# A two-layer graph network on one core: edge weights of the second layer by halves of the partitions, and one-hot products for more blocks of edges

## The chip, the core and the metric

The kernel runs on one NeuronCore of a Trainium2 chip. The core has five engines, each with its own instruction queue, which meet only through semaphores: TensorE (PE in the profile; its weight loads are listed apart as PEld), VectorE (DVE), ScalarE (ACT), GpSimd (POOL) and SyncE (SP), which here only issues transfers. TensorE writes to PSUM, which has eight banks of 2 KB per partition. The metric is the device time of the whole program in microseconds; the time before is the median of three runs.

## The reference

There are 6,250 nodes with 128 features and 200,000 directed edges, sorted by their receiving node. Each layer is added to its input.

```python
h = maximum(layernorm(x), 0)
# layer one: attention over the incoming edges, 8 heads of 16
z = (h @ W).reshape(N, 8, 16); el = einsum(z, attn_l); er = einsum(z, attn_r)
e = leaky_relu(el[src] + er[dst]);  a = exp(e - segment_max(e, dst)[dst])
x = x + segment_sum(z[src] * a, dst) / segment_sum(a, dst) + bias

h = maximum(layernorm(x), 0)
# layer two: s are the first 32 features, v the other 96 as 32 x 3
s, v = s @ W_up_s / sqrt(32), einsum(v, W_up_v) / sqrt(32)
t = silu(silu(edge_attr_8 @ A1 + b1) @ A2 + b2) @ A3        # 128 weights per edge
w0, w1, w2, w3 = split(t, 4)
m = concat(s[src] * y_s * w0, (v[src] . y_v) / sqrt(3) * w3,
           s[src] * y_v * w1, v[src] * y_s * w2)             # 256 per edge
x = x + (segment_sum(m, dst) / 10) @ W_out
```

Everything is float32.

## The kernel before

**Tiles and blocks.** 128 edges are a tile, one edge per partition; 16 tiles (KB) are a block. There are 1,563 tiles in 98 blocks (NB), the last of 11 tiles. Block b writes to a window of 128 nodes, of which the first 64 are complete when it ends; the other half is carried to the next block (`carry`). Two blocks complete one tile of 128 nodes, of which there are 50 (NX).

**Rows of the source nodes.** Each tile needs, for each of its 128 edges, the row of its source node: 136 numbers from table t0 in layer one, 128 from t1 in layer two. There are three ways to get them.

- A *gather*: one indirect DMA per tile, issued by GpSimd (`gather`, line 839).
- *By row*: for the last tile of every third block, SP issues 128 small DMAs with addresses from registers (`rows_by_row`, line 1154). ScalarE copies the result to its place (`filled`).
- *Products*: for the tile before the last (KD) of the blocks in `dense` (layer one, line 1200) or `dense1` (layer two, line 1201), TensorE multiplies one-hot matrices by a copy of the whole table that lies in SBUF as three bfloat16 parts (`t0s`, `t1s`). That takes 51 matmuls (`rows_of`, line 1313; `dense_rows`, line 1917), two wide comparisons on VectorE and three operations that pick the right range.

In layer one the copy of the table is read back in 17 chunks of three node tiles: `asked(k)` issues the DMA on SP, and `split(k)` makes the three parts on VectorE. Both have two buffers.

**The prologue.** Node tiles are loaded in ten groups, normalised, transposed and multiplied by W to give t0. Most of the normalising subtraction is on VectorE; in the groups before the last two, some tiles are given to GpSimd (line 960). The first KX = KB + 9 = 25 tiles of edges are gathered from x itself, before t0 is there (line 905), and go through the same arithmetic again, tile by tile (`rows_of` of the prologue with `raw`).

**Layer one** runs a loop over groups g (a group is a block; the last block is two). Step g works on the logits of block g, on the weights and sums of block g - 1 (`sums`, line 1427), and on the rows of blocks g + 1 and g + 2. At the end of each odd block a node tile is finished, and its rows are written to t1 (line 1495) and, all but the last three node tiles, to a second table t1z.

**Between the layers.** The first NE = 24 tiles of layer two are gathered from t1z, which lacks the last three node tiles, so they need not wait for them. `late_ends` and `late_rows` add what is missing by one-hot matmuls, four tiles at a time. All later gathers need t1 complete.

**Layer two** runs a loop over steps of four tiles (`us`), four per block. In step i of block b the order is:

1. at a block's start: gathers of block b + 2, rows of `filled`, features and attributes of block b + 2 (`edge_rows`: ft and yb), node rows;
2. `network(b + 1, ...)`: one of four parts of the two-layer network of the next block, through bank p_h (lines 1770 and 1774, Silu on ScalarE);
3. `tensor_weights` of step i + 1: two tiles of edges share the 128 partitions of h2, 64 each, so that one matmul per pair with a block-shaped a3p of 256 columns gives the weights p_w of both (line 1787); ScalarE scales two quarters of them (line 1791);
4. `messages` of step i on VectorE, lines 1807 to 1816;
5. products for this or the next block (`dense_step`), late rows, the one-hot matrix `s` of step i + 1;
6. if the step before ended a block: `finish` (VectorE adds the carry, ScalarE copies the next one), and one step later `node1`;
7. `sums1` of step i (line 1824), into bank p_u.

The order on PE, VectorE, ScalarE and SP is as written, by hand (`manual_schedule`). GpSimd issues nothing but gathers, into a ring of five buffers of a block each (`buffers`), plus z_first. In layer two p_h, p_w and p_u have two banks each, p_x and p_i one.

Of the kernel before, what the change touches and what calls it, by code (L numbers as in the profile page):

```python
# [9 lines left out]
F32 = mybir.dt.float32  # L10
# [3 lines left out]
OP = mybir.AluOpType  # L14
# [4 lines left out]
P = 128  # L19
# [5 lines left out]
MU = 32  # L25
# [716 lines left out]
def tile_even_edges(  # L742
# [62 lines left out]
    ok_i = keep.tile([1, 1], I32, name="fok")  # L805
    KX = KB + 9
    z_second = keep.tile([P, KB, ZW], F32, name="fz_second")
# [48 lines left out]
    with tc.manual_schedule(engines={mybir.EngineType.PE, mybir.EngineType.DVE,  # L856
# [81 lines left out]
        def rows_of(gx, xs, fp, fp_ps, raw=None):  # L938
# [5 lines left out]
            for k in range(NC + 3):  # L944
# [3 lines left out]
                if 0 <= c < NC:  # L948
                    i, n = gx[c]
                    rs, mr = rss[c], mrs[c] = normal(fp, mvs[c], rss[c], n, f"x{mark}{i}")  # L950
                    h = hs[c] = fp.tile([P, 6, P], F32, name="fh")
                    for j in range(n):
                        by = (i + j) % 7
                        if by in ((2, 6) if c < NC - 2 else (2,)):
                            nc.scalar.activation(h[:, j, :], xs[c][:, j, :], AF.Identity,
                                                 bias=mr[:, j, :], scale=rs[:, j, :])
                        else:
                            late = by in (0, 3, 5) and NC - 4 <= c < NC - 2 and not raw
                            eng = nc.gpsimd if late else nc.vector
                            eng.tensor_scalar(h[:, j, :], xs[c][:, j, :], mvs[c][:, j, 0:1],  # L960
                                              rs[:, j, :], op0=OP.subtract, op1=OP.mult)
                if k == NC + 1 and not raw:
# [48 lines left out]
def even_edges(tc, v):  # L1011
# [8 lines left out]
    with ExitStack() as ctx:  # L1020
# [27 lines left out]

        NL, NE = 3, 24
        LATE = NX - NL  # L1050
# [81 lines left out]
        a1p = const.tile([P, KB // 2, P], F32, name="fa1p")  # L1132
        nc.sync.dma_start(a1p, v["a1p"])
        a2p = const.tile([P, P], F32, name="fa2p")
# [43 lines left out]
        def finish(b, p_u, width, carry, agg, pool):  # L1178

            if b % 2 == 0:  # L1180
                agg = pool.tile([P, MW], F32, name="agg")
            o = agg[b % 2 * WB : b % 2 * WB + WB, :width]
            if carry is None:
                nc.vector.tensor_copy(o, p_u[:WB, :width])
            else:
                nc.vector.tensor_add(o, p_u[:WB, :width], carry[:, :width])
            carry = pool.tile([WB, MW], F32, name="carry")
            nc.scalar.copy(carry[:, :width], p_u[WB:, :width])
            return carry, agg

# [8 lines left out]
        TS = 3  # L1199
        dense = set(range(-(-NX // TS) + 4, NB - 4))  # L1200
        dense1 = set(range(10, NB - 4, 4))

# [35 lines left out]
        with tc.manual_schedule(engines=in_order), \  # L1238
# [338 lines left out]
            for g in range(NG - 3):  # L1577
# [5 lines left out]
                for n in split_:  # L1583
                    parts_out(n)
                asked(g - 2)
                if g % 2 == 0 and g // 2 + 2 < NX - 2:
# [68 lines left out]
                if to:  # L1655
                    rows_of(n2, 6, half - 6)
                split(g - 3)
                if g == 4:
# [76 lines left out]
        with tc.manual_schedule(engines=in_order), \  # L1735
# [11 lines left out]
            def edge_rows(b):  # L1747
                if b < NB:
                    c = blk[b]
                    c["ft"] = l1.tile([P, P], F32, name="ft", bufs=4)  # L1750
                    nc.sync.dma_start(c["ft"], f8[:, b, :])
                    c["yb"] = l1.tile([P, KB, 4], F32, name="yb", bufs=4)
                    nc.sync.dma_start(c["yb"], y4[:, b * KB : (b + 1) * KB, :])

            def network(b, step):

                c = blk[b]
                q0, second = step // 2 * 4, step % 2
                if 2 * q0 >= KT[b]:
                    return  # L1760
                if step == 0:
                    c["h2"] = []
                if step == 3 or 2 * q0 + 8 >= KT[b] and second:
                    c["yp"] = held[:, P + b % 2 * KB * 3 : P + (b % 2 + 1) * KB * 3].rearrange(
                        "p (t i) -> p t i", i=3)
                    nc.scalar.copy(c["yp"], c["yb"][:, :, 1:4])  # L1766
                p_h = l1_ps.tile([P, 4, P], F32, name="p_h")
                if not second:
                    for q in range(4):
                        nc.tensor.matmul(p_h[:, q, :], a1p[:, q0 + q, :], c["ft"], start=True, stop=True)  # L1770
                    c["h1"] = l1.tile([P, 4, P], F32, name="h1")
                    nc.scalar.activation(c["h1"], p_h, AF.Silu, bias=b1)  # L1772
                else:
                    nc.tensor.matmul(p_h.rearrange("p q e -> p (q e)"), a2p,  # L1774
                                     c["h1"].rearrange("p q e -> p (q e)"), start=True, stop=True)
                    h2 = l1.tile([P, 4, P], F32, name="h2", bufs=5)
                    nc.scalar.activation(h2, p_h, AF.Silu, bias=b2)  # L1777
                    c["h2"].append(h2)

            def tensor_weights(u):  # L1780

                b, k0, m = u["b"], u["k0"], u["m"]
                c = blk[b]
                w = u["w"] = l1_ps.tile([P, 4, 4, MU], F32, name="p_w")
                for k in range(0, m, 2):
                    q, n = (k0 + k) // 2, min(2, m - k)
                    nc.tensor.matmul(w[:, k : k + n].rearrange("p k a u -> p (k a u)"),  # L1787
                                     c["h2"][q // 4][:, q % 4, :],
                                     a3p[:, :n].rearrange("p k f -> p (k f)"), start=True, stop=True)
                for k in range(m):  # L1790
                    nc.scalar.activation(w[:, k, ::2, :], w[:, k, ::2, :], AF.Copy,  # L1791
                                         scale=c["yb"][:, k0 + k, 0:1])

            def messages(u):
                b, k0, m, w = u["b"], u["k0"], u["m"], u["w"]
# [67 lines left out]
            def late_ends(t):  # L1863

                if t < NE:
                    p_h = l1_ps.tile([P, 4, P], F32, name="p_h")
                    for k in range(4):
# [60 lines left out]
            def dense_step(b, q):  # L1928
# [6 lines left out]
                if b in dense1:  # L1935
# [17 lines left out]

            rows, rows_until.n, late, x_of = rows_by_row(1, t1, P), 0, [], {}
            for b in range(2):
                edge_rows(b)
                take_rows(b)
# [8 lines left out]
            carry = agg = None  # L1966
            ends = None
            for i, u in enumerate(us):
                b, k0, m = u["b"], u["k0"], u["m"]
                if k0 == 0:  # L1970
                    take_rows(b + 2)
                    filled(1, b, blk[b]["z"], P)
                    edge_rows(b + 2)
                    if b % 2 == 0:
                        node_rows1(b // 2, 1 if b < NB - 2 else 2)
                    table_tiles(b)
# [8 lines left out]
                late_ends(4 * (i + 2))  # L1985
                messages(u)
                if i == 26:
# [30 lines left out]
            nc.vector.tensor_copy(m_t[:, 2:], p_n[:, 2:])  # L2018
            p_o = l1_ps.tile([P, 4, P], F32, name="p_w")
            for j in range(2):  # L2020
                for q in range(2):
                    nc.tensor.matmul(p_o[:, j, :], m_t[:, 2 * j + q, :], wout[:, q, :],  # L2022
                                     start=q == 0, stop=q == 1)
            x_i = x_of[NX - 2]
            nc.vector.scalar_tensor_tensor(x_i, p_o[:, :2], POST, x_i, op0=OP.mult, op1=OP.add)  # L2025
            nc.sync.dma_start(out[first:].rearrange("(j p) f -> p j f", p=P), x_i)
# [138 lines left out]
```

## Time and profile before

| What | Value |
|---|---|
| three runs | 3743.76, 3744.0, 3754.08 us (median 3744.0) |
| the profiled execution | 3749.37 us, span 3747.6 us |
| last gather of layer one's last block ends | 1840.4 us |
| first gather from t1 | 1876.6 us |
| last sums of block 97 end | 3739.1 us |
| gathers on GpSimd | 2,971, of which 25 from x and 24 from t1z |
| matmuls and weight loads on PE | 19,845 each |
| mean granted clock of PE | 0.94; 0.64 to 0.73 between 150 and 400 us, 0.93 and more after 450 us |

The busy shares of the page are means over the whole span. How PE stands against GpSimd differs by stage, so it is read from windows and from the timeline. A float32 product is two matmul instructions with a weight load each; a matmul's duration in the profile includes its way through the array, so the pitch from one start to the next says what it costs in a row of them.

### The profile page before, as it was taken

The page shows a single profiled execution, that of the slowest core. Times are in us where ns is not written, and L with a number is a line of the kernel's source. Part 1 is how long each engine was busy: PE and PEld are TensorE (multiplying, and loading weights), DVE is VectorE, ACT ScalarE, POOL GpSimd, SP SyncE. Part 2 cuts the span into 40 slices and gives each one's busy share as a digit, 9 for nine tenths or more (in the row PEclk, how much of TensorE's full clock was granted, in tenths as well). Part 3 has the DMA queues.
Part 4 walks back from the last instruction along what each step waited for, and adds up shares of the span by engine and source line. Part 5 has one row for each costly group of instructions (what it writes and reads, how often), then busy time and mean ns, then how long its engine had stood idle before and what let it go on. Part 6 is the DMA issues. An engine that isn't in the chain of part 4 may idle for free. (4 is left out here: it accounts for less than half of the span.)

```text
span 3747.6 us, 74803 instructions
## 1 busy us (share of the span) xinstructions
PE 3196.4 (85%) x19845; PEld 2474.1 (66%) x19845; DVE 2633.1 (70%) x6272; ACT 1406.0 (38%) x3638; POOL 2817.3 (75%) x2981
## 2 busy tenths in 40 slices
PE   4756788888888888888788899999999999999997
PEld 4655566666666666666666677777677777767775
DVE  7755666666666666666657777777777777777776
ACT  4432333333333333333334444444444444444443
POOL 7777777777777777777777777777777777777776
PEclk7766899999999999999799999999999999999999
DMA  6333332222222222222223222222222222222222
GB/s 167 75 78 79 71 68 67 68 69 68 68 68 68 68 68 67 69 69 67 71 70 95 69 64 64 64 64 64 64 64 64 65 63 64 65 63 64 63 68 52
DMA packets 212534, 262.78 MB, mean 70 GB/s; under 512 B 77425, under 2 KB 163921, under 8 KB 212097
## 3 DMA queue, kind: packets, MB, share of 16 engines
q0 software_dynamic: 95072, 200.78, 22.6%
q1 hardware_dynamic: 116592, 57.03, 5.7%
q8 instruction: 159, 2.61, 0.3%
q14 instruction: 279, 2.28, 0.2%
q10 hardware_dynamic: 432, 0.09, 0.0%
HBM read 236.19 MB, written 21.14 MB: 69 GB/s over the span
## 5 line engine op out<-in xcount | busy, mean ns | idle before, releaser
L839 POOL DMA_INDIRECT fz<-ft,fsrc x1750 | 1654.1, 945 | 539.5 <-issue 327.0
L1824 PE MATMUL p_u<-mj,s 128*128 128x256 f32 x3126 | 764.3, 388 | 87.5 <-DVE mj L1816 86.5
L1313 PE MATMUL p_x<-t0s,fz_first 128*128 128x408 bf16 (+1 forms) x3723 | 730.0, 346 | 0.0
L1824 PEld LDWEIGHTS p_u<-mj,s 128*128 128x128 f32 x3126 | 582.2, 192 | 215.6 <-DVE mj L1816 139.7
L839 POOL DMA_INDIRECT fz_other<-ft,fsrc x589 | 557.2, 946 | 179.6 <-issue 107.6
L839 POOL DMA_INDIRECT fz_second<-ft,fsrc x583 | 554.0, 950 | 178.3 <-issue 107.9
L1313 PEld LDWEIGHTS <-fz_first 128*128 128x128 bf16 x3723 | 361.5, 101 | 231.5 <-issue 17.4
L1791 ACT ACTIVATE p_w<-p_w,yb 128x64 f32<-128x64 f32 x1563 | 451.5, 289 | 117.3 <-PE p_w L1787 73.8
L1787 PE MATMUL p_w<-fa3p,h 128*128 128x256 f32 x1564 | 408.4, 384 | 0.0
L1787 PEld LDWEIGHTS p_w<-fa3p,h 128*128 128x128 f32 x1564 | 286.7, 193 | 114.5 <-issue 48.8
L1772 ACT ACTIVATE h<-p_h,fb 128x512 f32<-128x512 f32 x196 | 134.7, 687 | 585.8 <-PE p_h L1770 575.1
L1337 ACT COPY mk<-p_m 128x384 f32<-128x384 f32 (+1 forms) x99 | 47.4, 479 | 658.5 <-PE p_m L1333 651.6
L1427 PE MATMUL p_u<-fz,s 128*128 128x136 f32 x1846 | 272.9, 308 | 20.1 <-DVE fz L1422 20.1
L1427 PEld LDWEIGHTS p_u<-fz,s 128*128 128x128 f32 x1846 | 258.5, 216 | 23.8 <-DVE fz L1422 22.2
L1173 DVE TENSOR_TENSOR s<-p_i,fdloc 128x512 f32<-128x512 f32 x391 | 268.6, 687 | 3.8 <-ACT p_i L1766 3.8
L1173 DVE TENSOR_TENSOR s<-p_m,fdloc 128x512 f32<-128x512 f32 x391 | 266.2, 682 | 3.0 <-ACT mk L1337 2.7
L1770 PE MATMUL p_h<-ft,fa1p 128*128 128x128 f32 x1568 | 216.1, 282 | 56.5 <-DMA ft<-in_e_f_dram 56.3
L1770 PEld LDWEIGHTS p_h<-ft,fa1p 128*128 128x128 f32 x1568 | 208.7, 197 | 79.8 <-issue 55.7
L1348 ACT CAST d<-p_d 128x512 bf16<-128x512 f32 x391 | 229.3, 586 | 78.0 <-PE p_d L1346 34.2
L1378 DVE TENSOR_TENSOR_SCAN pe<-mk,pe 128x128 f32<-128x128 f32 x98 | 42.0, 428 | 290.8 <-PE pe L1293 271.6
L1777 ACT ACTIVATE h<-p_h,fb 128x512 f32<-128x512 f32 x196 | 134.7, 687 | 260.4 <-PE p_h L1774 260.4
L1811 DVE TENSOR_REDUCE vd<-vy 128x128 f32<-128x384 f32 x391 | 229.6, 587 | 0.0
(285 smaller groups left out, 4880.5 us busy)
## 6 DMA issues: line engine op xcount, KB each, us to landing
r<-ft SPq DMA_DIRECT2D x3968, 0.5 KB
r<-ft SPq DMA_DIRECT2D x3840, 0.5 KB
fz<-ft,fsrc POOLq DMA_INDIRECT x1750
fz_other<-ft,fsrc POOLq DMA_INDIRECT x589
fz_second<-ft,fsrc POOLq DMA_INDIRECT x583
fx<-x SPq DMA_DIRECT2D x47, 160.0 KB
ft<-in_e_f_dram SPq DMA_DIRECT2D x98, 64.0 KB
t1s<-fx SPq DMA_DIRECT2D x7, 576.0 KB
```

The costliest lines, as they stand in the source:

```text
L839: nc.gpsimd.indirect_dma_start(out=to[:, k, :width], out_offset=None, in_=table, in_offset=bass.IndirectOffsetOnAxis(ap=src_col[:, t : t + ...
L1173: nc.vector.tensor_tensor(s[:, :m], iota[:, None, :].to_broadcast([P, m, P]), dloc[:, t : t + m].unsqueeze(2).to_broadcast([P, m, P]), OP. ...
L1313: nc.tensor.matmul(c["p_x"][:, :m, :], c["oh", k // half][:, k % half, :], t0s[:, i::NR, s, :], start=k == 0 and s == 0, stop=k == NR - 1 ...
L1348: nc.scalar.copy(d[:, :m], p_d[:, :m])
L1427: nc.tensor.matmul(c["p_u"][:, :ZW], c["s"][k // 4][:, k % 4, :], c["z"][:, k, :], start=c["o"] + k == 0, stop=c["o"] + k == KT[c["b"]] - 1)
L1770: nc.tensor.matmul(p_h[:, q, :], a1p[:, q0 + q, :], c["ft"], start=True, stop=True)
L1772: nc.scalar.activation(c["h1"], p_h, AF.Silu, bias=b1)
L1777: nc.scalar.activation(h2, p_h, AF.Silu, bias=b2)
L1787: nc.tensor.matmul(w[:, k : k + n].rearrange("p k a u -> p (k a u)"), c["h2"][q // 4][:, q % 4, :], a3p[:, :n].rearrange("p k f -> p (k f) ...
L1791: nc.scalar.activation(w[:, k, ::2, :], w[:, k, ::2, :], AF.Copy, scale=c["yb"][:, k0 + k, 0:1])
L1811: nc.vector.tensor_reduce(vd, vy.rearrange("p t i u -> p t u i"), AX.X, OP.add)
L1824: nc.tensor.matmul(blk[b]["p_u"][:, :MW], u["s"][:, k, :], u["mj"][:, k, :], start=k0 + k == 0, stop=k0 + k == KT[b] - 1)
```

## The change

It does the following.

- **Weights by halves** (layer two). a1p is loaded with its columns in another order (four DMAs for one), so that h2 holds tile t in half t // 2 % 2 of the partitions, and tiles 0 and 1 of a step in the same half. `tensor_weights` makes one matmul per tile, on 64 partitions, with 128 columns. Their order alternates the halves (tiles 0, 2, 1, 3), and p_w has two banks per step, tiles 0 and 1 in one, 2 and 3 in the other. With two buffers p_w takes four banks; p_h and p_u have one each.
- **Products** for more blocks: layer one from block 12 (was 21) to 93; layer two for b % 9 in 1, 3, 5, 7 between 10 and 93, 38 blocks (was every fourth from 10, 21 blocks).
- **The table's copy in layer one** is asked for at twice the rate: chunks 2g - 4 and 2g - 3 are asked for at the start of group g and split at its end. Before, chunk g - 2 was asked for and g - 3 split.
- **Layer norm**: the six tiles on GpSimd go to VectorE.
- **KX** is 29 instead of 25, **NE** is 28 instead of 24.
- **edge_rows** is called for block b + 3 instead of b + 2, with five buffers instead of four.
- **Block's end** (layer two): ScalarE copies the carry at the head of the next step; VectorE adds within `messages`, after five of its seven operations; before, both came after the one-hot matrix.
- The last step, of three tiles, becomes one of two and one of one.

```diff
-    KX = KB + 9
+    KX = KB + 13
...
-                            late = by in (0, 3, 5) and NC - 4 <= c < NC - 2 and not raw
-                            eng = nc.gpsimd if late else nc.vector
-                            eng.tensor_scalar(h[:, j, :], xs[c][:, j, :], mvs[c][:, j, 0:1],
-                                              rs[:, j, :], op0=OP.subtract, op1=OP.mult)
+                            nc.vector.tensor_scalar(h[:, j, :], xs[c][:, j, :], mvs[c][:, j, 0:1],
+                                                    rs[:, j, :], op0=OP.subtract, op1=OP.mult)
...
-        NL, NE = 3, 24
+        NL, NE = 3, 28
...
-        nc.sync.dma_start(a1p, v["a1p"])
+        halves = [a.rearrange("p (u k) (q f) -> p u k q f", k=2, q=2) for a in (a1p, v["a1p"])]
+        for k in range(2):
+            for q in range(2):
+                nc.sync.dma_start(halves[0][:, :, q, k, :], halves[1][:, :, k, q, :])
...
-        dense = set(range(-(-NX // TS) + 4, NB - 4))
-        dense1 = set(range(10, NB - 4, 4))
+        dense = set(range(-(-NX // TS // 2) + 3, NB - 4))
+        dense1 = {b for b in range(10, NB - 4) if b % 9 % 2}
...
-                asked(g - 2)
+                for k in range(2):
+                    asked(2 * g - 4 + k)
...
-                split(g - 3)
+                for k in range(2):
+                    split(2 * g - 4 + k)
...
-                    c["ft"] = l1.tile([P, P], F32, name="ft", bufs=4)
+                    c["ft"] = l1.tile([P, P], F32, name="ft", bufs=5)
...
-                p_h = l1_ps.tile([P, 4, P], F32, name="p_h")
+                p_h = l1_ps.tile([P, 4, P], F32, name="p_h", bufs=1)
...
-                w = u["w"] = l1_ps.tile([P, 4, 4, MU], F32, name="p_w")
-                for k in range(0, m, 2):
-                    q, n = (k0 + k) // 2, min(2, m - k)
-                    nc.tensor.matmul(w[:, k : k + n].rearrange("p k a u -> p (k a u)"),
-                                     c["h2"][q // 4][:, q % 4, :],
-                                     a3p[:, :n].rearrange("p k f -> p (k f)"), start=True, stop=True)
+                p_w = l1_ps.tile([P, 4, 2 * P], F32, name="p_w")
+                w = u["w"] = p_w[:, :, :P].rearrange("p k (a u) -> p k a u", u=MU)
+                for t in sorted(range(k0, k0 + m), key=lambda t: t % 2):
+                    q, half_t = t // 4 * 2 + t % 2, t // 2 % 2
+                    on = slice(64 * half_t, 64 * half_t + 64)
+                    nc.tensor.matmul(p_w[:, t - k0, :P], c["h2"][q // 4][on, q % 4, :], a3p[on, half_t],
+                                     start=True, stop=True)
...
+                between()
                 nc.vector.tensor_mul(mj[:, :, :MU], s_n, w[:, :m, 0, :])
...
-                    blk[b]["p_u"] = l1_ps.tile([P, 512], F32, name="p_u")
+                    blk[b]["p_u"] = l1_ps.tile([P, 512], F32, name="p_u", bufs=1)
...
+            if us[-1]["m"] > 2:
+                n = us[-1]["m"] - 2
+                us[-1]["m"] = 2
+                us.append({"b": NB - 1, "k0": us[-1]["k0"] + 2, "m": n})
...
+            def block_ended():
+                nonlocal carry, agg, ends
+                if ends is not None:
+                    agg = finish(ends, blk[ends]["p_u"], MW, carry, agg, l1n)
+                    carry = to_carry
+                    if ends % 2 == 1:
+                        done.append((ends // 2, agg))
+                    ends = None
...
+                if ends is not None:
+                    to_carry = l1n.tile([WB, MW], F32, name="carry")
+                    nc.scalar.copy(to_carry, blk[ends]["p_u"][WB:, :MW])
...
-                    edge_rows(b + 2)
+                    edge_rows(b + 3)
...
-                messages(u)
+                messages(u, block_ended)
...
-                if ends is not None:
-                    carry, agg = finish(ends, blk[ends]["p_u"], MW, carry, agg, l1n)
-                    if ends % 2 == 1:
-                        done.append((ends // 2, agg))
-                    ends = None
```

More of the change, by code (lines that the diff above doesn't have):

```diff
@@ L1186, in finish @@
                 nc.vector.tensor_add(o, p_u[:WB, :width], carry[:, :width])
-            carry = pool.tile([WB, MW], F32, name="carry")
-            nc.scalar.copy(carry[:, :width], p_u[WB:, :width])
-            return carry, agg
+            return agg
         NR = -(-NX // 3)
@@ L1749, in edge_rows @@
                     c = blk[b]
-                    c["ft"] = l1.tile([P, P], F32, name="ft", bufs=4)
+                    c["ft"] = l1.tile([P, P], F32, name="ft", bufs=5)
                     nc.sync.dma_start(c["ft"], f8[:, b, :])
-                    c["yb"] = l1.tile([P, KB, 4], F32, name="yb", bufs=4)
+                    c["yb"] = l1.tile([P, KB, 4], F32, name="yb", bufs=5)
                     nc.sync.dma_start(c["yb"], y4[:, b * KB : (b + 1) * KB, :])
@@ L1792, in tensor_weights, with messages @@
                                          scale=c["yb"][:, k0 + k, 0:1])
-            def messages(u):
+            def messages(u, between=lambda: None):
                 b, k0, m, w = u["b"], u["k0"], u["m"], u["w"]
@@ L1865, in late_ends @@
                 if t < NE:
-                    p_h = l1_ps.tile([P, 4, P], F32, name="p_h")
+                    p_h = l1_ps.tile([P, 4, P], F32, name="p_h", bufs=1)
                     for k in range(4):
@@ L1954, in even_edges @@
             rows, rows_until.n, late, x_of = rows_by_row(1, t1, P), 0, [], {}
+            for b in range(3):
+                edge_rows(b)
             for b in range(2):
-                edge_rows(b)
                 take_rows(b)
@@ L2018, in even_edges @@
             nc.vector.tensor_copy(m_t[:, 2:], p_n[:, 2:])
-            p_o = l1_ps.tile([P, 4, P], F32, name="p_w")
+            p_o = l1_ps.tile([P, 4, 2 * P], F32, name="p_w")
             for j in range(2):
                 for q in range(2):
-                    nc.tensor.matmul(p_o[:, j, :], m_t[:, 2 * j + q, :], wout[:, q, :],
+                    nc.tensor.matmul(p_o[:, j, :P], m_t[:, 2 * j + q, :], wout[:, q, :],
                                      start=q == 0, stop=q == 1)
             x_i = x_of[NX - 2]
-            nc.vector.scalar_tensor_tensor(x_i, p_o[:, :2], POST, x_i, op0=OP.mult, op1=OP.add)
+            nc.vector.scalar_tensor_tensor(x_i, p_o[:, :2, :P], POST, x_i, op0=OP.mult, op1=OP.add)
             nc.sync.dma_start(out[first:].rearrange("(j p) f -> p j f", p=P), x_i)
```

## The prediction

> **What bounds the kernel.** I read the page's busy shares first, then the windows view, then GpSimd's timeline. The page names no clear bound, since PE, VectorE and GpSimd all stand between 70 and 85%:
>
> ```profile
> PE 3196.4 (85%) x19845; PEld 2474.1 (66%) x19845; DVE 2633.1 (70%) x6272; ACT 1406.0 (38%) x3638; POOL 2817.3 (75%) x2981
> L839 POOL DMA_INDIRECT fz<-ft,fsrc x1750 | 1654.1, 945 | 539.5 <-issue 327.0
> ```
>
> The second line shows that a gather is 945 ns with 0.30 us of idle "issue" in front of it: one per 1.248 us. GpSimd at 75% is therefore full. The windows view (columns: window, length, then busy us and count of PE, PEld, DVE, ACT, POOL; PE clock; DMA) agrees, with 240 to 242 gathers in every 300 us (300/1.248 = 240):
>
> ```profile
> 700.00:1000.00 300.00, 265.60 (x2072) 196.26 (x2072) 202.94 (x424) 92.79 (x213) 226.81 (x241) 0.95 0.30 68
> 2400.00:2700.00 300.00, 272.46 (x1358) 210.96 (x1357) 225.84 (x560) 131.55 (x368) 226.77 (x241) 1.00 0.25 64
> ```
>
> Only two places interrupt that stream, both in GpSimd's timeline (start, duration, what, idle before):
>
> ```profile
> 24.10 4.21 POOL L960 TENSOR_SCALAR fh<-fxs,mvx,rsx 128x128 f32<-128x128 f32 x5 [0.46 <-PE p_t L975]
> 28.47 1.03 POOL L905 DMA_INDIRECT fz_second<-in_e_xp_dram,frow  x1 [0.16 <-issue]
> ...
> 1869.61 0.94 POOL L839 DMA_INDIRECT fz<-ft1z,fsrc  x1 [0.31 <-issue]
> 1876.60 0.94 POOL L839 DMA_INDIRECT fz<-ft,fsrc  x1 [6.04 <-PE p_h L1868]
> ```
>
> The first is the layer norm on GpSimd. The second is the wait for table t1 to be complete: its last write is issued by SP at 1873.8, after layer one's last block.
>
> GpSimd is not alone. Setting each block's last gather against its last sum (p_u matmuls of L1427, L1824), I find in layer one, where every block has products, 18.77 us per block for PE (blocks 24 to 88) against 18.35 for the gathers: PE falls behind, and the time by which a buffer is free before its refill shrinks from 35 to 8 us. In layer two PE enters 60 us behind the gathers (block 3 summed at 1984.9, gathered by 1925.0), takes 18.58 per block (10 to 92) against 19.2, and has caught up only at block 92; block 97's sums end at 3739.1. So the end belongs to GpSimd, but PE has almost nothing to give. In layer two PE's pace is its own: two blocks without products take 15.06 (odd) and 17.11 (even, with the node step), mean 16.09; one with products adds 51 matmuls of L1917 at 0.162 = 8.3. At one in four that is 18.16; the missing 0.42 is mostly the wait for ft, 56.3 us in 36 waits. PE's and SP's timelines show one:
>
> ```profile
> 2629.02 1.13 PE L1770 MATMUL p_h<-ft,fa1p 128*128 128x128 f32 x8 [1.97 <-DMA ft<-in_e_f_dram]
> 2403.95 0.37 SPq L1751 DMA_DIRECT2D ft<-in_e_f_dram  x1
> 2404.42 0.39 SPq L1753 DMA_DIRECT2D yb<-in_e_y_dram  x1
> 2409.33 12.97 SPq L1154 DMA_DIRECT2D r<-ft  x32
> ```
>
> SP is never idle here: rows for one block in three make 18.6 us per block, and ft stands behind them.
>
> **The gathers.** Products replace one gather per block: nine more blocks in layer one (12 to 20), 17 more in layer two (38 instead of 21). Layer two: 17 x 1.248 = **21.2 us** off GpSimd after t1. Layer one: 11.2, and 4.5 from the layer norm leaving GpSimd (28.47 back to 23.95; the six rows cost VectorE, whose L960 is some 0.28 each, 1.7 us on the way to t0, which the four added x-gathers cover). But these 15.7 us count only if t1 is ready earlier, and that is PE's end of layer one. NE = 28 puts four more gathers before the wait: 4 x 1.248 = **5.0** off what follows it.
>
> **Is layer one's end earlier?** Blocks 12 to 20 go from the gathers' 19.6 to PE's 18.77: up to 9 x 0.8 = 7, with 4.5 from the start. Against it stands the table's copy in SBUF: now asked for one group ahead, after the change two chunks asked and split in the same group. In group 10 the split ran at 244.6 on VectorE, while SP reached its request of that group only at 247.79, behind rows. So VectorE will wait there: request 247.8 + 5 (the extra requests at 0.45 on a full SP, and the bias of its start) + 3 landing + two splits of 2.3 = 260, where group 10 ended at 247. From there PE runs at 18.77 with no slack: group 25 ends at 260 + 15 x 18.77 = 542, where block 24 ended at 541.1. I take **no gain** at t1 (ends: 11 earlier if SP is in time, 6 later).
>
> GpSimd then ends at 3739.1 - 21.2 - 5.0 = **3713** (in terms of the last sums). It can hold 15.7 us more of lead only up to the 8 us of free buffers; after that it waits for PE, at no cost.
>
> **PE in layer two.** Let s be what the weights stage saves per four tiles. Now it is four matmul instructions at 216 ns, 0.87 us (2601.47 to 2602.34). After, eight of 128 columns on 64 rows, alternating halves, each half to its own bank. The trace has no two halves side by side. Nearest rows, in PE's timeline:
>
> ```profile
> 1015.37 0.36 PE L1391 MATMUL pe<-mx,fshift 128*128 128x1 f32 x2
> 1015.59 0.36 PE L1393 MATMUL pe<-mx,fshift 128*128 128x1 f32 x2
> ...
> 1852.83 0.37 PE L1388 MATMUL pe<-mx,fshift 64*64 64x1 f32 x2
> 1853.13 0.37 PE L1391 MATMUL pe<-mx,fshift 24*64 24x1 f32 x2
> 1853.42 0.37 PE L1393 MATMUL pe<-mx,fshift 64*64 64x1 f32 x2
> ```
>
> The first two: matmuls of one column still stand 0.11 apart, because each carries an fp32 load of 128 weight columns. If the loads of both halves go one after the other, eight cost 8 x 0.112 = 0.89 and nothing is won. Against that the Trainium skill, "TensorEngine Tiling (Array Packing)", Key Properties, says that different tiles load weights and multiply in parallel: then 4 x 0.112 = 0.45. But "TensorE: Matmul & The Clock Gate", Part 3, says matmuls start and end strictly in order; each fp32 product is two instructions on one half, so only the second of one overlaps the first of the next: five slots, 0.56. And the tiling page's rule that speaks against the change: a switch of tiling mode drains TensorE. By the rule alone a drain is the 0.16 us by which a 128-column matmul (275 ns) outlasts its 112 ns slot, twice per four tiles: 0.32. By the row it is less: 64*64 to 24*64 and back is 170 ns from the last start to the next, against 128 inside a pair, at half clock: 0.04, so 0.08 twice. The row decides. Ends: s from -0.11 (serial, plus switches) to 0.34. I take the middle of the two side-by-side cases, 0.60: **s = 0.27**.
>
> PE's end: block 0 ended at 1927.3; a late step more (a four-tile step with late rows took about 10 us, one without 4) and p_h with one buffer: +8, 1935. Blocks 1 to 9: 9 x (16.09 - 4s) + 10. Blocks 10 to 92: 83 x (16.09 + 8.3 x 4/9 + 0.1 - 4s). The last five 80 - 19s. Sum **3820 - 387 s** = 3715 at s = 0.27. The 0.42 of waits is gone, as ft comes a block earlier; 0.1 stands for the single p_u bank: its first sum waits for VectorE's add, now in the middle of messages(), and for the carry copy at the head of ScalarE's queue, behind which the Silu waits; PE has the next network and weights (1.4 us) meanwhile, the add and what is behind it 1.3. VectorE carries 12.8 + 0.6 + 3.6 x 4/9 = 15 us per block, under PE's 18.8. The a1p load in four pieces (1 us more of SP at 45 us) lies before rows that wait for 50.7; the last step split in two trades 0.8 us of PE for 0.8 of VectorE.
>
> GpSimd 3713, PE 3715: the end moves from 3739.1 to **3715, -24 us**. Span 3747.6 to 3724, the profiled 3749.4 to 3725; it stands 5.4 above the median, so 3744 becomes **3720**.
>
> **Rivals.** (1) *The halves don't overlap*, because weight loads serialise: s = -0.11 to 0, end 3820 to 3862, time 3825 to 3867. For it: the 0.11 us rows. Against: the tiling rule. It decides below s = 0.21, where PE alone ends later than 3739. Chance 0.17, slower. (2) *Overlap, but a switch costs the whole tail*: s about 0.12, end 3773, time 3778 (3750 to 3800); chance 0.15, of which 0.06 no change. (3) *SP is in time*, and layer one ends 11 us earlier, with s of at least 0.3: 3702, time 3707; chance 0.10. The forecast has 0.58 with its own range 3705 to 3733 (0.02 of it no change). Within 0.3%, 11 us, a measurement can't tell it from no change. Faster 0.56 + 0.10 = 0.66; same 0.08; slower 0.09 + 0.17 = 0.26. The range takes in (3) and most of (2), up to 3790, and leaves out (1).
>
> **What would show it.** Right: 26 gathers fewer, still 1.248 apart; eight p_w matmuls in some 0.6 us from the first to what follows; no ft waits; blocks without products in 14 to 16 us; the t1 gathers again near 1876; the last gather close before the end. Wrong: p_w matmuls 0.11 apart, layer two's gathers waiting for PE's buffers, the last sums long after the last gather; or t1 written near 1865.

## The result, and the profile after

The changed kernel takes **3854.0 us** (median of four runs, 3846.1 to 3871.9) against 3744.6 before: a ratio of 1.029 with a 95% interval of 1.025 to 1.033. It is slower by 2.9%, where 3720 was forecast. The profiled execution, the slowest of the four, took 3871.9 us with a span of 3870.1.

From the busy shares of the page of the changed kernel:

```profile
PE 3358.8 (87%) x22829; PEld 2527.8 (65%) x22829; DVE 2732.6 (71%) x6431; ACT 1398.3 (36%) x3643; POOL 2789.3 (72%) x2950
```

GpSimd does 28 us less work, as intended, and TensorE 162 us more. From the windows view of the changed kernel (columns as before the change: window, length, then busy us and count of PE, PEld, DVE, ACT, POOL; PE clock; DMA):

```profile
2400.00:2700.00 300.00, 276.46 (x1687) 205.08 (x1687) 219.86 (x536) 122.12 (x346) 226.50 (x241) 0.99 0.25 64
3000.00:3300.00 300.00, 272.83 (x1646) 202.26 (x1646) 214.48 (x522) 119.00 (x337) 210.44 (x224) 0.97 0.23 59
3600.00:3870.00 270.00, 238.56 (x1430) 177.39 (x1428) 196.18 (x493) 107.96 (x307) 131.15 (x139) 0.97 0.17 43
```

The reader should look at the count of GpSimd: 241 gathers in 300 us at first, 224 later. The stream that set the end before now waits for buffers. Its last gather ends at 3777.2, the last sums at 3861.5, 84 us later. Layer two belongs to TensorE. Yet TensorE is idle there for about a tenth of the time, so the first question is what it waits for; the second, taken up with e2, is why its granted clock is 0.97 in the later windows. From its waits after 1960 us (what waited, for what; us in total, times, longest), first before the change, then after:

```profile
PE p_u L1824 <- DVE mj L1816: 77.2, 102, 3.7
PE p_h L1770 <- DMA ft<-in_e_f_dram: 52.8, 35, 4.4
PE p_i L1838 <- ACT m_t L1836: 26.0, 47, 1.4
PE p_i L1834 <- DVE s L1173: 17.6, 24, 1.9
```

```profile
PE p_u L1830 <- DVE mj L1822: 84.7, 105, 1.9
PE p_i L1840 <- DVE s L1175: 60.7, 27, 3.2
PE p_i L1844 <- ACT m_t L1842: 26.2, 48, 1.1
```

The waits for ft are gone, as predicted. In their place stands the second line: the node step's transposes (`node1`) wait for a one-hot matrix, up to 3.2 us at a time. Nothing in the prediction speaks of it. TensorE's and VectorE's timelines of the changed kernel show one such place (start, duration, what, idle before and what ended it):

```profile
3355.17 0.72 PE L1793 MATMUL p_w<-fa3p,h 64*128 64x128 f32 x8
3355.82 0.49 PE L1909 MATMUL p_x<-fident,key 128*128 128x128 f32 x2
3359.49 0.44 PE L1840 MATMUL p_i<-fident,agg 128*128 128x128 f32 x2 [3.18 <-DVE s L1175]
3360.39 1.12 PE L1844 MATMUL p_i<-fwout,m_t 128*128 128x128 f32 x4 [0.46 <-ACT m_t L1842]
```

```profile
3355.07 0.55 DVE L1822 TENSOR_TENSOR mj<-fz_other,p_w 128x384 f32<-128x384 f32 x1
3356.34 2.49 DVE L1913 TENSOR_TENSOR ohs<-p_x,place_r 128x1152 bf16<-128x1152 f32 x2 [0.73 <-PE p_x L1909]
3358.75 0.68 DVE L1175 TENSOR_TENSOR s<-p_i,fdloc 128x512 f32<-128x512 f32 x1
3361.61 0.29 DVE L1845 SCALAR_TENSOR_TENSOR x<-p_i,x 128x128 f32<-128x128 f32 x1 [2.17 <-issue]
```

VectorE has finished the messages, waits 0.73 us for the key matmul of the products, makes the two row comparisons of `dense_ends` (2.49 us), and only then the one-hot (L1175). The one-hot reads iota_p. In the code iota_p and p_n, into which the transposes write, are parts of the same PSUM bank, p_i; that explains why TensorE waits for an operation whose result it does not need here. The Trainium skill, "PSUM — Partial Sum Buffer", section "PSUM bank collisions raise a hardware error", asks that PSUM be guarded by bank and quadrant of partitions (or simply by bank) and not by address; the release in this trace fits that. A run with iota_p in another bank was not made.

Why was it rare before? A node step falls into step 1 of an even block. The row comparisons for block b + 1 fall into step 1 of block b. Before, all blocks with products were even (10, 14, ...), so their comparisons were made in odd blocks and the two never met. With b % 9 in 1, 3, 5, 7, 18 of the 38 blocks are odd. In the trace of the changed kernel exactly 18 node steps come right behind a key matmul, and the first transpose starts 3.45 us, on average, after the second of the key matmul's two instructions.

The time from the last sum of one block to that of the next (p_u matmuls) gives the size. Before the change, an odd block without products took 15.06 us and an even one 17.11. After: 14.66 and 16.98. A pair with products in its even block takes 18.49 + 20.78 = 39.27, a pair with products in its odd block 43.7 to 44.8.

### The profile page after: what moved, and what is told of

Same layout as the page of the kernel before. It is cut to its first block, busy times and chain, and to the rows that moved or that the text cites. A ratio compares the mean times of both kernels' runs of the same rounds, so it can differ in the third digit from the quotient of the medians.

```text
span 3870.1 us, 80984 instructions
## 1 busy us (share of the span) xinstructions
PE 3358.8 (87%) x22829; PEld 2527.8 (65%) x22829; DVE 2732.6 (71%) x6431; ACT 1398.3 (36%) x3643; POOL 2789.3 (72%) x2950
## 5 line engine op out<-in xcount | busy, mean ns | idle before, releaser
L839 POOL DMA_INDIRECT fz<-ft,fsrc x1730 | 1635.3, 945 | 577.7 <-issue 334.6
L1830 PE MATMUL p_u<-mj,s 128*128 128x256 f32 x3126 | 787.3, 396 | 100.6 <-DVE mj L1822 95.1
L1313 PE MATMUL p_x<-t0s,fz_first 128*128 128x408 bf16 (+1 forms) x4182 | 812.8, 344 | 0.0
L1830 PEld LDWEIGHTS p_u<-mj,s 128*128 128x128 f32 x3126 | 591.6, 197 | 212.3 <-DVE mj L1822 111.0
L1313 PEld LDWEIGHTS <-fz_first 128*128 128x128 bf16 x4182 | 403.5, 100 | 255.9 <-issue 14.4
L1923 PE MATMUL p_x<-t1s,ohs 128*128 128x384 bf16 (+1 forms) x1938 | 341.9, 324 | 0.0
L1793 PEld LDWEIGHTS p_w<-fa3p,h 64*128 64x128 f32 x3126 | 205.1, 186 | 173.4 <-issue 150.1
L1793 PE MATMUL p_w<-fa3p,h 64*128 64x128 f32 x3126 | 280.2, 297 | 0.0
L1175 DVE TENSOR_TENSOR s<-p_i,fdloc 128x512 f32<-128x512 f32 x392 | 265.9, 678 | 4.9 <-DMA r<-ft 4.9
L1175 DVE TENSOR_TENSOR s<-p_m,fdloc 128x512 f32<-128x512 f32 x391 | 265.6, 681 | 2.7 <-ACT mk L1337 2.0
L1923 PEld LDWEIGHTS <-ohs 128*128 128x128 bf16 x1938 | 174.0, 98 | 117.8
L1300 DVE TENSOR_TENSOR fz_first<-pe,place_r 128x1152 bf16<-128x1152 f32 (+1 forms) x164 | 211.0, 1287 | 27.7 <-ACT mx L1382 27.0
```

The lines of the kernel that those rows point to most:

```text
L839: nc.gpsimd.indirect_dma_start(out=to[:, k, :width], out_offset=None, in_=table, in_offset=bass.IndirectOffsetOnAxis(ap=src_col[:, t : t + ...
L1175: nc.vector.tensor_tensor(s[:, :m], iota[:, None, :].to_broadcast([P, m, P]), dloc[:, t : t + m].unsqueeze(2).to_broadcast([P, m, P]), OP. ...
L1300: nc.vector.tensor_tensor(oh[:, :n], c["at"].unsqueeze(1).to_broadcast([P, n, P]), ranges[2][:, h * half : h * half + n].unsqueeze(2).to_b ...
L1313: nc.tensor.matmul(c["p_x"][:, :m, :], c["oh", k // half][:, k % half, :], t0s[:, i::NR, s, :], start=k == 0 and s == 0, stop=k == NR - 1 ...
L1793: nc.tensor.matmul(p_w[:, t - k0, :P], c["h2"][q // 4][on, q % 4, :], a3p[on, half_t], start=True, stop=True)
L1830: nc.tensor.matmul(blk[b]["p_u"][:, :MW], u["s"][:, k, :], u["mj"][:, k, :], start=k0 + k == 0, stop=k0 + k == KT[b] - 1)
```

## The experiments

The first theory is this meeting of two jobs. Its rivals: each block with products costs the same wherever it lies; the weights' halves save too little; layer one ends later (its last sums end at 1875.4 in the profiled execution, 9.4 later than before).

**e1_even: the meeting avoided by parity.**

```diff
-        dense1 = {b for b in range(10, NB - 4) if b % 9 % 2}
+        dense1 = set(range(18, NB - 4, 2))
```

> The changed kernel, with layer two's products in the 38 even blocks 18 to 92 instead of the 38 blocks with remainder 1, 3, 5 or 7 by nine: as many products, as many gathers. Theory 1 (two jobs meet): where an odd block has products, its row comparisons (2.49 us on VectorE) are made in the same step of the even block before it as the node step; the one-hot of that step comes behind them, and the node's transposes on TensorE, which share a PSUM bank with what the one-hot reads, wait about 3.2 us. A pair of blocks takes 44.5 us with products in the odd one and 39.3 in the even one, so 18 odd ones cost 18 x 5.2 = 94 us: about 3770 (3755 to 3790). Theory 2 (each block with products costs the same wherever it lies, and the loss is the weights stage and the number of products): 3854 plus or minus 12.

3794.0 us (ratio to before 1.0124, 1.0094 to 1.0153): 60 us less than the changed kernel in the medians, 80 in the profiled executions (3791.6 against 3871.9). Theory 2 falls. The pairs take 39.27 us (median), as computed; blocks 10 to 17, now without products, gain less than computed, because TensorE waits there for ft again (17.4 us in 7 waits between 2080 and 2240). The time is just outside the 3755 to 3790 expected.

**e2_onehot_first: the meeting kept, the order on VectorE turned.**

```diff
+                if i + 1 < NU:
+                    n = us[i + 1]
+                    n["s"] = one_hot(n["b"] * KB + n["k0"], n["m"], iota_p, l1s)
                 dense_step(b, k0 // 4)
                 late_rows(4 * (i + 1))
-                if i + 1 < NU:
-                    n = us[i + 1]
-                    n["s"] = one_hot(n["b"] * KB + n["k0"], n["m"], iota_p, l1s)
```

> The changed kernel with its own blocks, only the one-hot of the next step issued ahead of the row comparisons on VectorE. Theory 1 (the transposes wait for the one-hot behind the comparisons): the wait of some 3.2 us in front of the transposes falls below 1 us, 18 times, and the time to about 3795 (3770 to 3815). Theory 2 (the transposes wait for the sums before them or for the comparisons themselves, or what they lose is lost at the next wait for messages): no gain, 3854 plus or minus 12.

**3723.8 us** (0.9945, 0.9925 to 0.9965): 130 us less than the changed kernel, and 0.5% faster than the kernel before. This gain is larger than either theory expected, since the wait is not the only thing that goes. TensorE's waits after 1960 us in this kernel:

```profile
PE p_u L1830 <- DVE mj L1822: 43.8, 82, 1.9
PE p_i L1844 <- ACT m_t L1842: 31.6, 47, 0.9
PE p_i L1840 <- DVE s L1175: 3.7, 10, 0.4
```

The wait in question fell from 60.7 to 3.7 us, and the waits for messages from 84.7 to 43.8. The same place in the two timelines of this kernel, TensorE's and then VectorE's:

```profile
3285.25 0.49 PE L1909 MATMUL p_x<-fident,key 128*128 128x128 f32 x2
3285.69 0.44 PE L1840 MATMUL p_i<-fident,agg 128*128 128x128 f32 x2
3286.97 0.71 PE L1844 MATMUL p_i<-fwout,m_t 128*128 128x128 f32 x4 [0.84 <-ACT m_t L1842]
```

```profile
3284.96 0.68 DVE L1175 TENSOR_TENSOR s<-p_i,fdloc 128x512 f32<-128x512 f32 x1
3285.77 2.49 DVE L1913 TENSOR_TENSOR ohs<-p_x,place_r 128x1152 bf16<-128x1152 f32 x2
3288.18 0.28 DVE L1845 SCALAR_TENSOR_TENSOR x<-p_i,x 128x128 f32<-128x128 f32 x1
```

The one-hot now lies in the 0.73 us in which VectorE waited for the key matmul anyway, and the transposes run beside the comparisons. A pair with products in the odd block takes 19.80 + 18.61 = 38.41 us, one with products in the even block 17.89 + 20.01 = 37.90 (medians). Against the changed kernel that is 18 x 5.8 + 20 x 1.37 = 132 us: the whole difference in the medians of the runs. The order thus costs something in pairs without the meeting too.

The waits alone don't add up to that. TensorE's waits after 1960 us come to 173 us in the changed kernel and 86 here, 87 less. The rest is TensorE's clock. The sums behind the transposes and a stretch of the windows view around them, in the changed kernel:

```profile
3361.30 3.20 PE L1830 MATMUL p_u<-mj,s 128*128 128x256 f32 x8
3360.00:3365.00 5.00, 4.61 (x18) 4.02 (x19) 3.38 (x9) 0.33 (x1) 3.78 (x4) 0.66 0.33 87
```

The same in e2:

```profile
3287.52 1.89 PE L1830 MATMUL p_u<-mj,s 128*128 128x256 f32 x8
3285.00:3290.00 5.00, 4.16 (x29) 3.45 (x28) 4.87 (x9) 1.82 (x6) 3.78 (x5) 1.00 0.19 53
```

At each of the 18 meetings the changed kernel's trace has a stretch of 3.4 or 6.8 us at half clock, 102 us in all. Between 1960 us and the last sums it has no others, and e2's trace has none at all there. An estimate, from the pitches in these stretches against the pitches of the same matmuls at full clock, puts their cost at 39 us. With the 87 us of waits that is 126, of 128 by which layer two, from block 0's last sum to block 97's, is shorter in the profiled executions (1918.8 and 1791.0 us).

**e3_full_rows: the weights by whole partitions**, `tensor_weights` and the load of a1p as before the change, all else as changed.

> The changed kernel with the edge weights by whole partitions again: four matmul instructions of 256 columns per four tiles, as before the change, all else as changed. In the changed kernel's trace the stage takes 0.65 us from the first p_w matmul to what follows and its first one starts 93 ns late: 0.745 us, so it saves 0.12 against 0.863 (theory 1): 387 steps x 0.12 = 46 us slower, 3900 (3885 to 3915). If it saves nothing because other waits set the pace (theory 2): 3854 plus or minus 10. If it saves the 0.27 of the prediction: 3958.

3867.4 us (1.0321, 1.0295 to 1.0347): 13 more than the changed kernel, between the two theories, with intervals that overlap. Blocks without products show the full size: 15.06 instead of 14.66 for odd ones, 17.37 instead of 16.98 for even ones, 0.10 us per step of four tiles. But the pairs with products in the odd block take 24.55 + 19.73 = 44.28 us, no more than with halves. TensorE's waits after 1960 us come to 153 us, 20 less than in the changed kernel, and half clock costs 27 by the same estimate, 12 less: most of the 46 us goes there. So the halves can be judged only without the wait, in e5.

**e4_layer1_back: layer one undone**, products from block 21, the table asked for and split once per group.

> The changed kernel with layer one undone: products from block 21, one chunk of the table asked for and split per group. The changed kernel's last sums of layer one end at 1875.4 against 1866.0, and nine of these are lost by block 8 already. Theory 1 (the doubled requests and splits delay the first groups, and TensorE never makes it up): layer one ends 9 earlier, all of it seen at the end because layer two is TensorE's: 3845 (3840 to 3850). Theory 2 (the extra gathers of x and the layer norm on VectorE are the delay): 3854 plus or minus 4.

3855.0 us (1.0282, 1.0251 to 1.0313): no difference in the medians, though the start of layer one is as theory 1 says: block 9's sums end at 244.4 us here, at 269.3 in the changed kernel (249.6 before). VectorE waits there for the chunk it splits, as the waits of the changed kernel from 100 to 280 us show, where the trace of before has no such wait:

```profile
DVE t0s L1228 <- DMA zr<-ft: 8.2, 3, 4.8
```

What is lost there is within what the same layer-one program varies by: in nine profiled executions with the changed layer one (the changed kernel, e1 to e3, e5 to e7, f1, f2) its last sums end between 1851.4 and 1875.4 us, median 1858.9. In the five with layer one undone or as before the change (before, e4, e8, f3, f4) they end between 1855.5 and 1866.4, median 1866.0. The 1875.4 of the changed kernel is the latest of all, so the third rival falls. Theory 2's number came, but what it names as the delay was not tried alone.

Four runs on the base of e2 then priced the parts with the wait gone.

**e5_full_onehot: e2 with the weights by whole partitions** (the edits of e2 and e3 together).

> e2_onehot_first with the edge weights by whole partitions again, so what the halves bring once the wait is gone. Theory 1 (the halves save 0.10 us per step of four tiles, as the blocks without products show: 15.06 against 14.66 us for four steps, and TensorE is on the path): 387 x 0.10 = 39 us, less the few us by which TensorE may trail: 3755 (3745 to 3765). Theory 2 (with the wait gone GpSimd alone sets the end, the weights are hidden): 3724 to 3730.

3753.6 us (1.0017, 1.0007 to 1.0028), 30 more than e2: theory 1. That is 0.08 us per step over the whole run, and 0.10 in blocks without products (15.06 against 14.66). Without the halves the rest is no gain.

**e6_ft_late: e2 with ft and yb as before the change.**

```diff
-                    edge_rows(b + 3)
+                    edge_rows(b + 2)
...
```

> e2_onehot_first with ft and yb asked for two blocks ahead in four buffers, as before the change, instead of three ahead in five. Theory 1 (the 56 us of waits for ft in the trace of before were real, and TensorE is on the path): 25 to 50 us slower, 3750 to 3775. Theory 2 (TensorE makes up for them against the gathers, as it seems to have done before): 3724 to 3735.

3735.6 us (0.9975, 0.9965 to 0.9985), 12 more than e2: just above theory 2's range. The waits for ft do not come back as they were: there are five, 13.8 us together, all between block 5 and block 12, where the kernel before had 36 over the whole of layer two. Blocks 1 to 9 take 176.9 us instead of 156.4, blocks 10 to 92 no longer than in e2 (1555.3 and 1558.2). With products in four blocks of nine, ft is late only at the start.

**e7_by_half: e2 with both tiles of the lower half first.**

```diff
-                for t in sorted(range(k0, k0 + m), key=lambda t: t % 2):
+                for t in sorted(range(k0, k0 + m), key=lambda t: t // 2 % 2):
```

> e2_onehot_first with the weights of a step in another order: both tiles of the lower half first, then both of the upper half. Theory 1 (matmuls start in program order, so only neighbours on different halves run side by side): seven slots of 0.107 in place of four, 0.3 us more per step of four tiles, blocks without products 14.66 + 1.2 us, and 387 x 0.3 = 116: 3830 (3790 to 3850). Theory 2 (each half has a queue of its own and the order does not matter): 3724 plus or minus 6, the starts still in pairs 7 ns apart.

3725.2 us (0.9934, 0.9907 to 0.9960): theory 2. The starts are still in four pairs, now 14 ns apart instead of 7. Strict starting order, as theory 1 and the prediction took it, would give seven slots here; the measurement has four.

**e8_before_rows: the kernel before, with the new `dense1`, ft and yb three blocks ahead and the one-hot first.**

> The kernel before the change with three things of the whole: products in the 38 blocks with odd remainders by nine, ft and yb three blocks ahead, and the one-hot ahead of the row comparisons. Weights by whole partitions, two buffers each for p_h and p_u, layer one as before. Theory 1 (the gain is products for gathers, with the weights' halves a side matter worth 0.10 per step, of which the single p_u buffer takes back 0.03): TensorE ends at 3713 + 39 - 13 - 8 = 3731, GpSimd at 3695 + 5 to 10: 3742 (3730 to 3750). Theory 2 (without the halves TensorE cannot carry 38 blocks of products): 3765 or more.

3747.7 us (1.0012, 1.0002 to 1.0022): theory 1. As in e5, more products without the halves bring no gain.

**The last four** were run twice. The first time (e9_node_later, e10_node_more, e11_before_odd, e12_layer1_back) they fell on a chip on which the kernel before itself took 5902 us, with a mean clock of 0.79 and long idle times on all engines; there they were slower than the kernel before by 0.4 to 1.7%. Why that chip is so slow the traces don't say, and a gain of 0.5% measured elsewhere need not hold on it. The second time they ran beside a kernel before of 3743.7 us.

**f3_before_odd: the kernel before, its products moved by one block.**

```diff
-        dense1 = set(range(10, NB - 4, 4))
+        dense1 = set(range(11, NB - 4, 4))
```

> The kernel before the change, only its 21 blocks with products in layer two moved by one, from 10, 14, ... to 11, 15, ...: odd blocks, whose row comparisons fall into the node step's step. Theory 1 (the meeting costs some 4.6 us a time, 44.3 against 39.7 us per pair): 21 x 4.6 = 96 us of TensorE, of which waits for ft (56 us) may take up a part: 3785 (3775 to 3840). Theory 2 (it costs only in the changed kernel): 3744 plus or minus 5.

3779.1 us (1.0093, 1.0077 to 1.0110): theory 1. As many products and gathers, nothing else changed, and 35 us slower. TensorE's waits after 1960 us in this kernel, against those of before above:

```profile
PE p_i L1834 <- DVE s L1173: 82.8, 46, 3.2
PE p_u L1824 <- DVE mj L1816: 60.3, 76, 1.7
PE p_h L1770 <- DMA ft<-in_e_f_dram: 17.9, 6, 5.5
```

The transposes' wait rises from 17.6 to 82.8 us, 21 of the transposes starting 3.45 us after the key matmul's second instruction. The waits for ft fall from 52.8 to 17.9, so that all waits together are only 12 us longer than before (187 and 175). Half clock makes the larger part: it comes at each of the 21 meetings, and by the same estimate costs 53 us against 17 before. The meeting costs by itself.

**f4_layer1_back: e2 with layer one undone** (the edits of e2 and e4 together).

> e2_onehot_first with layer one undone (products from block 21, one chunk of the table per group). Theory 1 (layer one ends with TensorE, and its products from block 12 bring nothing): 3724 plus or minus 6. Theory 2 (GpSimd sets the end of layer one): nine gathers more, 3735.

3727.2 us (0.9949, 0.9929 to 0.9969): theory 1. Layer one's products from block 12 bring nothing that can be measured.

**f1_node_later and f2_node_more: can the rest of the node step be hidden too?** In f1 the add of x moves behind the next messages:

```diff
-                nc.vector.scalar_tensor_tensor(x_i, p_n[:, 0, :], POST, x_i, op0=OP.mult, op1=OP.add)
+                pending.append(x_i)
...
                 messages(u, block_ended)
+                nodes_added()
```

> e2_onehot_first, with the node step's last operation (the add of x on VectorE, which waits for TensorE's transposes and wout matmuls) issued one step later, behind the next messages. Theory 1 (VectorE stands still there for up to 3.8 us and TensorE then waits for the messages): TensorE ends up to 58 us earlier, GpSimd's 3695.5 and a trail of 6 us set the end: 3712 (3705 to 3717). Theory 2 (the node step's wait is TensorE's own, for m_t): 3724 plus or minus 5.

3722.7 us (0.9938, 0.9920 to 0.9956): theory 2, and the blocks of every kind take the same median time as in e2. f2 has products in all 42 even blocks besides (`b % 2 == 0`).

> f1_node_later with layer two's products in all 42 even blocks 10 to 92, four gathers fewer. Theory 1 (the order of the operations, not the parity or the number, was the loss, and GpSimd sets the end): 4 x 1.248 = 5 less than f1: 3707 (3700 to 3713). Theory 2 (TensorE sets the end): 4 x 6.3 = 25 more than f1.

3732.0 us (0.9957, 0.9941 to 0.9973): 9 more than f1, so TensorE sets the end, as in theory 2, but less than its 25: 18 blocks with products also move from odd to even, where a pair is 0.5 us shorter (37.90 against 38.41). So e2 is the version to keep; f1 and e7 can't be told from it. The single banks for p_h and p_u, the new order at a block's end, KX, NE and the layer norm were not undone one by one.

## Why the prediction was wrong

By its own steps, with the profiled execution of the changed kernel (last sums 3861.5, predicted 3715) and of e2 (3713.1) beside the sum:

| Part of the sum for PE, us | predicted | changed | e2 |
|---|---|---|---|
| block 0 ends | 1935 | 1942.7 | 1922.1 |
| blocks 1 to 9 | 145 | 157.2 | 156.4 |
| blocks 10 to 92 | 1560 | 1684.4 | 1558.2 |
| blocks 93 to 97 | 75 | 77.2 | 76.4 |

**The step that failed** is "Blocks 10 to 92: 83 x (16.09 + 8.3 x 4/9 + ...)". It charges a block with products the matmuls of L1917 and nothing else, wherever the block lies. In the changed kernel these 83 blocks took 1684.4 us, not 1560: a pair with products in its odd block takes 44.2 us, where two blocks without products take 31.6 and 8.3 more was charged. The prediction named the row comparisons only as a share of VectorE's busy time ("3.6 x 4/9", "15 us per block, under PE's 18.8"), that is as throughput, and did not ask what stands behind them on VectorE's queue. The line that showed the dependence was in the trace of before: the transposes' wait for a one-hot, 17.6 us in 24 waits. e2 puts the price of the order at 130 us, e1 and f3 show the place. Nor did the sum have a term for the clock: by the estimate above, some 39 of the 130 us are matmuls at half clock behind the waits.

**The weights' saving s was mis-sized**: 0.10 us, not 0.27. The starts of p_w at one step of the changed kernel (the one at 3355.17), in us from the start of the L1777 matmul pass ahead:

```
0.000  L1777, second pass
0.521, 0.529   first pair of p_w
0.735, 0.742   second pair
0.847, 0.854   third pair
0.959, 0.965   fourth pair
1.167  what follows (L1909)
```

The halves do run side by side, in four slots and not the five that the prediction took. But the first pair comes 0.092 later than a whole-row p_w did (0.429), the second is 0.214 behind it instead of 0.111, and what follows comes 0.202 to 0.208 after the last pair instead of about 0.11. So a visit to the halves costs 0.3 us besides its four slots: 0.646 + 0.092 = 0.74, against 0.863 before. Here the prediction weighed the tiling page's rule, that a switch of tiling mode drains TensorE (twice 0.16, its own estimate), against rows of L1388 and L1391 (twice 0.08), and let the row decide. The measured 0.3 is the rule's price, though these starts don't show whether a drain makes it. The rows were a poor neighbour: they switch from 64 rows to 24 and back among matmuls of one column at half clock, in a stretch where pitches are long anyway. Rival (2), with s = 0.12, had the size of s right, but not the time, since it didn't know the meeting either. The blocks without products give 0.10. Besides, the changed kernel loses 0.13 per block, where 0.1 was predicted for the single p_u bank: even blocks take 17.37 in e3 against 17.11 before, odd ones the same. Which part of the new block's end costs it was not tried.

**Two errors cancel in e2**, which lands within 4 us of the forecast. By the smaller s, blocks 10 to 92 should take 83 x 4 x 0.17 = 56 us more. But a block with products costs TensorE 6.3 to 6.8 us (37.90 and 38.41 less 14.66 + 16.98), not 8.3, which makes 37 x 1.8 = 67 less. At least part of that is matmuls that fill waits: TensorE's waits in a pair fall from 2.7 us without products to 1.8 and 1.3 with them. That e2 confirms the forecast's number is therefore no proof of its working.

**What held.** The ft waits went, though by e6 most of them went with the added products and not because ft comes a block earlier. The gathers stay 1.248 apart in e2, 241 in 300 us. Layer one's end brings no gain that can be measured; VectorE waits for the table's chunks as said, and block 9 ends at 269 where 260 was said of group 10. The first gather from t1 starts at 1885.8, "near 1876" only within the spread of these executions (1865.3 in e2, 1873.0 in e5). The signs listed for "wrong" came: the gathers wait for TensorE's buffers, and the last sums end long after the last gather.

## What to carry to other kernels

An operation added to an in-order queue is priced by what stands behind it and who waits for that, not by its share of the engine's time: here 2.5 us of comparisons on an engine with a quarter of its time free cost 130 us, and moving three lines gave them back. Where such a wait comes with a lower granted clock, as the 3.18 us waits did here, the matmuls behind it are dearer too, and a list of waits does not show that. Jobs that recur with different periods (every second block, four of nine) should be laid over each other step by step before the change, and the shared PSUM bank counts as a meeting too. Where a rule of the chip speaks against a change and the only row against the rule comes from other shapes at another clock, take the rule's price into the forecast beside the row's; here the rule's was the nearer.

## What the runs showed of the hardware

- A visit to 64-row matmuls between 128-row ones costs about 0.3 us (0.092 at the entry, 0.1 behind the first pair, 0.1 at the exit), for fp32 with 128 columns at a slot of 0.111 us. Of the 0.42 us that four slots should have saved, 0.10 to 0.12 are left.
- The order in which a step's matmuls are written for the two halves is of no account: alternating or one half first, 3723.8 and 3725.2 us. That the starts in a pair stand 7 and 14 ns apart fits halves that are fed separately; the trace doesn't name the half, so this is not shown.
- A wait of 3.18 us on TensorE came with half clock for 3.4 or 6.8 us: at 18 of 18 meetings in the changed kernel, 17 of 18 in e3, 21 of 21 in f3. In e2, without these waits, there was none between 1960 us and the last sums. The pitch of the sums behind the wait was up to 0.427 us instead of 0.216.
- The same program in layer one ends anywhere from 1851.4 to 1875.4 us in nine profiled executions. A change worth less than that there can't be read from one profile.
